# Two stacked graph-attention layers: three more turns by DRAM trips, a round over four graphs, edge counts on ScalarE

## The chip, the cores and the metric

The kernel runs on one core of a Trainium2 chip. The time is the device time of one execution in microseconds (us), the median of three runs. A core has TensorE (PE in the profile, with PEld for its weight loads), VectorE (DVE), ScalarE (ACT), GpSimd (POOL) and SyncE (SP, which here only issues DMAs). Each takes its instructions in program order and waits on semaphores for the others.

## The reference

64 graphs of 256 nodes with 512 features go through two attention layers, each with a layer norm and a ReLU ahead and a residual sum behind. The first layer is itself two attentions: four heads of 256, ELU, then one head of 512. The second has eight heads of 64. All of it is fp32.

```
h = maximum(layernorm(x), 0)
# layer 0: mask = (adj > 0) | eye
xl = h @ W1 ; e = leaky_relu(asrc[i] + adst[j], 0.2) ; attn = softmax over sources of e, masked
z = elu(attn^T @ xl + b1)                      # 4 heads x 256
x = x + (the same with W2, one head of 512, on z) + b2
h = maximum(layernorm(x), 0)
# layer 1: mask = adj > 0, softmax over the second index, 8 heads x 64
x = x + relu(attention(h @ W_proj))
```

## The kernel before

`short_path` does the work; `general_path` is a fallback that runs only if a range test at the end fails, and it does not run here. The graphs are independent. A class `Graph` holds the steps of one graph as methods, and a text named `order` lists the steps of one *round*; every round runs this list, where the number ahead of a step is the offset of the graph it works on ("-1 exp2" in round r is step exp2 of graph r-1). Scheduling is by hand: the list is the program order on every engine. Beside the B + 2 = 66 rounds there are pieces of weight preparation that are dealt out between the steps of rounds 0 and 1.

The steps are these.

- `load`, `stats1`, `norm1`: x and adj come in, VectorE takes mean and variance, GpSimd makes the scale and the offset, ScalarE writes the normed h.
- A left operand of TensorE must be turned (features on partitions). For the first product h goes to DRAM and comes back with its 32-row blocks regrouped (`away1`), then VectorE's 32x32 block transpose finishes the turn (`turn1`, in `back`). For the other two products TensorE itself transposes 128x128 squares through PSUM, and ScalarE moves them to SBUF (`turn2` on z, 16 squares for a graph; `turn3` on the second h, 8 squares).
- Each projection is a Strassen-Winograd product of 2x2 blocks (class `Product`): seven products p1 to p7, with sums of the left blocks by GpSimd (`left`). m1a and m1b are the two halves of h @ W1 (seven products of 4 matmul records each), m2 is z @ W2 (seven of 8), m3 is h @ W_proj (seven of 4). Products p1, p6, p7, p4 accumulate into one PSUM tile `sum`; after p1, p6 and p7 ScalarE copies it out (`kept`), and the next of them can't write before that copy is done. VectorE adds the copies to the other PSUM tiles (`put`, at c22, p2, p3).
- `exp1/2/3` makes the attention factors; they go to DRAM and come back broadcast to all partitions (`spread`). `edges1/2/3` makes one head's weights: ScalarE scales a broadcast row (`wy`), VectorE takes the maximum and the mask (`e`), twice a head.
- `gat1/2/3` multiplies weights and values on TensorE, `out1/2/3` divides by the sum. `out1` also starts the ELU with two ScalarE passes (`ez`: ReLU, Exp), and `elu1` ends it on VectorE.
- `masks` makes the mask of layer 0 and the caps a01 of layer 1 with the count of edges of each row, all on VectorE; `cap3` turns the caps by a DMA transpose.

Of the kernel before, what the change touches and what calls it, by code (L numbers as in the profile page):

```python
# [17 lines left out]
P = 128  # L18
# [19 lines left out]
class Product:  # L38
# [19 lines left out]
    def kept(self, name):  # L58
        s = self.work.tile([P, 268], F32, name=name)
        self.nc.scalar.activation(s[:, :self.n], self.sum[:, :self.n], AF.Copy)  # L60
        return s

    def p1(self):
        self.sum = self.ps_sum.tile([P, 512], F32, name="sum")
        self.product(self.sum, 0, True, False)
        self.s1 = self.kept("s1")
# [10 lines left out]
    def p6(self):  # L77
        self.product(self.sum, 2, False, False)
        self.u2 = self.kept("u2")

    def p7(self):
        self.product(self.sum, 4, False, False)
        self.u3 = self.kept("u3")
# [14 lines left out]
def short_path(ctx, tc, flags, x, adj, w1, att_src1, att_dst1, b1, w2, att_src2, att_dst2, b2, w_proj, w_att,  # L98
# [12 lines left out]
    G = 4  # L111
# [9 lines left out]
    ps_mm = ctx.enter_context(tc.tile_pool(name="ps_mm", bufs=4, space=PSUM))  # L121
    ps_tr = ctx.enter_context(tc.tile_pool(name="ps_tr", bufs=2, space=PSUM))
# [5 lines left out]
    ident = const.tile([P, P], F32, name="ident")  # L128
# [33 lines left out]
    class Norm:  # L162
# [10 lines left out]
        def end(self):  # L173
            ve = small.tile([P, 2, T], F32, name="ve")
            nc.vector.tensor_scalar(ve[:, 0, :], self.mv[:, :, 1], EPS, None, ALU.add)
            nc.vector.tensor_scalar(ve[:, 1, :], self.mv[:, :, 0], -1.0, None, ALU.mult)
            rstd = small.tile([P, T], F32, name="rstd")
            nc.gpsimd.tensor_tensor(rstd, ve[:, 0, :], neg_half, ALU.pow)
            off = small.tile([P, T], F32, name="off")
            nc.gpsimd.tensor_tensor(off, ve[:, 1, :], rstd, ALU.mult)  # L180
            return rstd, off
# [8 lines left out]
    def turn(h, c, pt):  # L190
        for k in range(2):
            for t in range(T):
                nc.tensor.transpose(pt[:, k, t * P:(t + 1) * P], h(t, c + k), ident)  # L193

    def away(h):

        kept = dram.tile([T, 4, P, P], F32, name="kept_h")
        nc.sync.dma_start(kept.rearrange("t a p e -> p t a e"), h.rearrange("p t (a e) -> p t a e", a=4))  # L200
        nc.sync.dma_start(h, kept.rearrange("t a (j q) e -> (a j) t (q e)", q=4))

    def back(h, a):

        for t in range(T):
            nc.vector.transpose(a[:, 4 * t:4 * t + 2].rearrange("p r k (j q) -> p q (r k) j", q=4),  # L206
                                h[:, t].rearrange("p (q c i) -> p q c i", q=4, c=4))
# [9 lines left out]
    def left_of(h, gone):  # L217

        a = work.tile([P, 7, DC // 2, P], F32, name="hs")
        if gone:  # L220
            back(h, a)
        else:
            for r in range(2):
                pt = ps_tr.tile([P, 2, N], F32, name="pt")
                turn(lambda t, c: h[:, t, c * P:(c + 1) * P], 2 * r, pt)
                nc.scalar.activation(a[:, r:r + 5:4], pt.rearrange("p k (t q) -> p t k q", t=T), AF.Copy)
# [3 lines left out]
    def spread(w, heads):  # L230

        kept = dram.tile([heads, P, T], F32, name=f"kept{heads}")
        nc.sync.dma_start(kept.rearrange("h p t -> p h t"), w)
        rows = []
# [41 lines left out]
    class Graph:  # L276


        def __init__(self, b):
            self.b = b  # L280

        def load(self):
            self.xs = io.tile([P, T, D], F32, name="xs")
# [4 lines left out]
        def masks(self):  # L288

            self.mask = work.tile([P, T, N], BF16, name="mask")  # L290
            nc.vector.scalar_tensor_tensor(self.mask, self.ad, 0.0, eye, ALU.is_gt, ALU.max)
            a01 = self.a01 = work.tile([P, T, N], BF16, name="a01", bufs=1)
            nc.vector.tensor_scalar(a01, self.ad, 0.0, None, ALU.is_gt)
            deg = small.tile([P, T], F32, name="deg")
            nc.vector.tensor_reduce(deg, a01, AX.X, ALU.add)
            none = small.tile([P, T], F32, name="none")
            nc.vector.tensor_scalar(none, deg, 0.5, EVEN, ALU.is_lt, ALU.mult)
            for t in range(T):
                nc.vector.tensor_scalar(a01[:, t, :], a01[:, t, :], OPEN, none[:, t:t + 1], ALU.mult, ALU.add)

        def stats1(self):
# [4 lines left out]

            exs = self.exs = small.tile([P, 6 * (H1 + 1 + H3)], F32, name="exs")
            self.ex1 = exs[:, :6 * H1].rearrange("p (i t) -> p i t", t=T)
            self.ex2 = exs[:, 6 * H1:6 * (H1 + 1)].rearrange("p (i t) -> p i t", t=T)
            self.ex3 = exs[:, 6 * (H1 + 1):].rearrange("p (i h t) -> p i h t", i=3, t=T)  # L310
# [7 lines left out]
        def away1(self):  # L318
            away(self.h)

        def turn1(self):
            a = left_of(self.h, True)
# [3 lines left out]
        def cap3(self):  # L326
            self.cap = work.tile([P, T, N], BF16, name="cap")
# [4 lines left out]
        def exp1(self):  # L332
            exps(lambda sl: self.ex1[:, sl].rearrange("p h t -> p t h"), H1, xl1[:, :, 0, :L1], xl1[:, :, 1, :L1])
            self.bc1 = spread(self.ex1[:, 2 * H1:], H1)
            self.zt = [work.tile([P, HF], F32, name=f"z{t}", bufs=1) for t in range(T)]
# [16 lines left out]
        def out1(self, g, t):  # L352
            z = self.zt[t]
            for h, pm in self.pms:
                r = small.tile([P, 1], F32, name="r1")
                nc.vector.reciprocal(r, pm[:, Q:Q + 1])
                sl = slice(h * F1, (h + 1) * F1)
                nc.vector.scalar_tensor_tensor(z[:, sl], pm[:, :Q], r, b1_sb[:, sl], ALU.mult, ALU.add)  # L358

            ez = work.tile([P, 2 * F1], F32, name="ez")  # L360
            nc.scalar.activation(ez, z[:, 2 * g * F1:2 * (g + 1) * F1], AF.Relu, scale=-1.0)  # L361
# [3 lines left out]
        def elu1(self, g, t):  # L365
            z = self.zt[t][:, 2 * g * F1:2 * (g + 1) * F1]
# [3 lines left out]
        def turn2(self, r, k):  # L370
            if r == 0 and k == 0:
                self.a2 = work.tile([P, 7, HC // 2, P], F32, name="h1s", bufs=1)
                self.m2 = Product(nc, ps_sum, ps_mm, work, self.a2, w2_sb, put2)
            pt = ps_tr.tile([P, 2, N], F32, name="pt")
            turn(lambda t, c: self.zt[t][:, c * P:(c + 1) * P], 4 * r + 2 * k, pt)
            nc.scalar.activation(self.a2[:, r:r + 5:4, 2 * k:2 * k + 2], pt.rearrange("p k (t q) -> p t k q", t=T),
                                 AF.Copy)
            if r == 1 and k == 1:
                left(self.a2, HC // 2)

        def exp2(self):
            exps(lambda sl: self.ex2[:, sl].rearrange("p h t -> p t h"), 1, xl2[:, :, 0, :L2], xl2[:, :, 1, :L2])
            self.bc2 = spread(self.ex2[:, 2:3], 1)
# [37 lines left out]

        def turn3(self):
            self.m3 = Product(nc, ps_sum, ps_mm, work, left_of(self.h, False), wp_sb, put3)

        def exp3(self):
# [6 lines left out]
            self.bc3 = spread(self.ex3[:, 2], H3)  # L432
# [15 lines left out]
        def out3(self, a, t):  # L448
# [3 lines left out]
            o = work.tile([P, G, K3], F32, name="o", bufs=4)  # L452
# [18 lines left out]
    def bring(w, src, at, r, by, squares=False):  # L471

        nk, n = w.shape[2], w.shape[3]
        for half in range(2):
            dst = blocks(w)[r][half][:, :, n - Q:]
            cols = src[:, at + half * Q:at + (half + 1) * Q]
            if squares:
                for a in range(4):
                    by[half].dma_start(dst[32 * a:32 * (a + 1)], cols[a * P:(a + 1) * P].rearrange(
                        "(c i) f -> i c f", c=4)[:, r * nk:(r + 1) * nk])  # L480
            else:
                by[half].dma_start(dst, cols.rearrange("(c p) f -> p c f", p=P)[:, r * nk:(r + 1) * nk])
# [385 lines left out]
```

## Time and profile before

| | |
|---|---|
| median of three runs | 3426.02 us (3424.45 to 3426.62) |
| profiled execution: device time | 3423.96 us |
| profiled execution: first to last instruction | 3421.9 us |
| VectorE busy | 2492.3 us, 73% of the span |
| ScalarE busy | 1876.7 us, 55% |
| GpSimd busy | 1231.4 us, 36% |
| DMA, mean share of the 16 engines | 3 tenths, 82 GB/s |

The times come from one profiled execution. "Busy" is the time in which at least one instruction of an engine runs. A group's mean is the length of one instruction; the starts of neighbours lie up to 0.09 us closer than these lengths, because instructions overlap at their ends. "Idle before" says how long the engine stood still ahead of an instruction, and who ended it.

### The profile page before, as it was taken

Reading aid. Unit: us, or ns where it says so; the run is one execution under the profiler, and the core shown is the slowest. Engines: PE = TensorE matmul, PEld = TensorE weight load, DVE = VectorE, ACT = ScalarE, POOL = GpSimd, SP = SyncE. Lnnn points to the kernel's source line nnn. Section 1 sums busy time; section 2 is a strip of 40 time slices with the busy share of each in tenths; the row PEclk is TensorE's granted clock in tenths of the full one; section 3 lists DMA queues with packets and bytes.
Section 4 is the critical chain, followed back from the end, with each engine's and each line's share of the span. In section 5 each row is a group of like instructions: output and inputs, shape, how many; then the busy total and the mean of one; then the engine's idle time right before and its main releaser. Section 6 shows DMA issues by size and latency. Waiting matters only on the chain.

```text
span 3421.9 us, 51905 instructions
## 1 busy us (share of the span) xinstructions
PE 3326.7 (97%) x17668; PEld 2899.3 (85%) x17668; DVE 2492.3 (73%) x6447; ACT 1876.7 (55%) x4481; POOL 1231.4 (36%) x1369
## 2 busy tenths in 40 slices
PE   4899999999999999999999999999999999999997
PEld 3688888888888888888888888888888888888886
DVE  7577777777777777777777777777777777777773
ACT  2355555555555555555565565565565565555553
POOL 1333433333433433433433433433433434334332
PEclk8999999999999999999999999999999999999997
DMA  4223323323223233323323323323223233232331
GB/s 134 58 85 82 82 85 81 83 82 85 83 80 86 81 81 83 85 78 81 90 75 82 92 75 82 90 76 83 86 80 83 81 86 81 80 87 78 84 78 40
DMA packets 354316, 280.87 MB, mean 82 GB/s; under 512 B 159616, under 2 KB 254848, under 8 KB 354048
## 3 DMA queue, kind: packets, MB, share of 16 engines
q1 hardware_dynamic: 352480, 275.40, 29.7%
q8 instruction: 144, 2.36, 0.3%
q10 hardware_dynamic: 1568, 2.10, 0.2%
q14 instruction: 124, 1.02, 0.1%
HBM read 201.07 MB, written 67.96 MB: 79 GB/s over the span
## 4 chain that ended last, share of the span: by engine, by line
PE 88%; ACT 5%; DMA 3%; DVE 2%; issue 1%; POOL 0%; SPq 0%; ACTq 0%; DVEq 0%
PE sum L54 30%; PE pm L54 21%; PE pm L445 13%; PE pm L348 13%; PE pm L399 6%; PE pt L193 5%; ACT wy L273 3%; DMA kept<-exs 1%; DMA bc<-kept 1%; ACT u L60 1%; ACT s L60 0%; DVE wy L492 0%; DMA w1a_sb<-in_L_gnn_W_dram 0%; DVE e L274 0%; POOL o L553 0%
## 5 line engine op out<-in xcount | busy, mean ns | idle before, releaser
L273 ACT ACTIVATE wy<-bc,exs 128x256 f32<-128x256 f32 x1664 | 768.9, 520 | 194.5 <-DMA bc<-kept 79.2
L455 POOL TENSOR_TENSOR x<-x,o 128x256 f32<-128x256 f32 x256 | 197.7, 772 | 1446.0 <-DVE o L453 1446.0
L274 DVE SCALAR_TENSOR_TENSOR e<-wy,exs,cap 128x256 f32<-128x256 f32 x1024 | 486.4, 511 | 141.0 <-ACT wy L273 133.3
L445 PEld LDWEIGHTS pm<-xl,e 128*128 128x128 f32 x4096 | 505.4, 195 | 26.5 <-issue 9.8
L348 PE MATMUL pm<-xl,e 128*128 128x257 f32 x2048 | 496.6, 385 | 9.9 <-DVE e L274 6.5
L445 PE MATMUL pm<-xl,e 128*128 128x65 f32 x4096 | 494.5, 275 | 11.3 <-DVE e L274 11.3
L54 PE MATMUL sum<-w_sb,h1s 128*128 128x257 f32 x2048 | 493.7, 383 | 0.7 <-ACT u L60 0.7
L54 PEld LDWEIGHTS sum<-w_sb,h1s 128*128 128x128 f32 x2048 | 379.9, 190 | 73.6 <-issue 21.8
L246 DVE TENSOR_TENSOR xl<-pm,u 128x256 f32<-128x256 f32 (+2 forms) x512 | 214.8, 419 | 310.0 <-PE pm L54 249.8
L348 PEld LDWEIGHTS pm<-xl,e 128*128 128x128 f32 x2048 | 375.2, 191 | 59.2 <-DVE e L274 8.4
L60 ACT ACTIVATE u<-sum 128x260 f32<-128x260 f32 (+3 forms) x512 | 196.5, 384 | 356.7 <-PE sum L54 350.7
L54 PE MATMUL pm<-w_sb,h1s 128*128 128x257 f32 x1536 | 365.0, 379 | 0.0
L54 PEld LDWEIGHTS pm<-w_sb,h1s 128*128 128x128 f32 x1536 | 290.9, 189 | 43.9
L54 PE MATMUL sum<-w1a_sb,hs 128*128 128x260 f32 x1024 | 274.7, 391 | 36.0 <-DVE hs L206 28.8
L274 DVE SCALAR_TENSOR_TENSOR e<-wy,exs,mask 128x256 f32<-128x256 f32 x640 | 274.7, 476 | 46.9 <-ACT wy L273 46.9
L212 POOL TENSOR_TENSOR hs<-hs 128x256 f32<-128x256 f32 x128 | 93.6, 731 | 543.1 <-DVE hs L206 324.6
L54 PE MATMUL sum<-wp_sb,hs 128*128 128x264 f32 x1024 | 277.3, 393 | 1.2 <-ACT u L60 1.1
L54 PE MATMUL sum<-w1b_sb,hs 128*128 128x256 f32 x1024 | 271.1, 387 | 1.0 <-ACT u L60 1.0
L54 PEld LDWEIGHTS sum<-w1a_sb,hs 128*128 128x128 f32 x1024 | 188.4, 190 | 89.2 <-ACT u L60 32.1
L358 DVE SCALAR_TENSOR_TENSOR z<-pm,r,b_sb 128x256 f32<-128x256 f32 x512 | 247.7, 484 | 18.1
L361 ACT ACTIVATE ez<-z 128x512 f32<-128x512 f32 x256 | 160.4, 627 | 164.9 <-DVE z L358 164.7
L399 PE MATMUL pm<-xl,e 128*128 128x257 f32 (+1 forms) x1024 | 243.8, 381 | 0.8 <-DVE e L274 0.7
(92 smaller groups left out, 5284.7 us busy)
## 6 DMA issues: line engine op xcount, KB each, us to landing
bc<-kept SPq DMA_DIRECT2D x384, 256.0 KB, 3.8
xs<-in_x_dram SPq DMA_DIRECT2D x64, 512.0 KB, 3.9
kept_h<-h SPq DMA_DIRECT2D x64, 512.0 KB, 3.2
h<-kept_h SPq DMA_DIRECT2D x64, 512.0 KB, 3.6
out_dram<-x SPq DMA_DIRECT2D x64, 512.0 KB, 2.8
ad<-in_adj_dram SPq DMA_DIRECT2D x64, 256.0 KB, 4.2
bc<-kept SPq DMA_DIRECT2D x64, 128.0 KB, 4.2
w_sb<-in_L_gnn_W_dram SPq DMA_DIRECT2D x4, 512.0 KB, 9.2
```

The lines of the kernel that those rows point to most:

```text
L54: self.nc.tensor.matmul(to[:, :self.n], self.lhs[:, i, c, :], self.rhs[:, i, c, :], start=(first and c == 0), stop=(last and c == self.nk ...
L60: self.nc.scalar.activation(s[:, :self.n], self.sum[:, :self.n], AF.Copy)
L193: nc.tensor.transpose(pt[:, k, t * P:(t + 1) * P], h(t, c + k), ident)
L246: nc.vector.tensor_tensor(dst, pm, add, ALU.add)
L273: nc.scalar.activation(wy, bc, AF.Copy, scale=yw)
L274: nc.vector.scalar_tensor_tensor(dst, wy.rearrange("p t q -> p (t q)"), xw, mask, ALU.max, op)
L348: nc.tensor.matmul(pm[:, :Q + 1], self.e[1, h][:, s, t * P:(t + 1) * P], xl1[:, s, h, L1:], start=(s == 0), stop=(s == T - 1))
L358: nc.vector.scalar_tensor_tensor(z[:, sl], pm[:, :Q], r, b1_sb[:, sl], ALU.mult, ALU.add)
L361: nc.scalar.activation(ez, z[:, 2 * g * F1:2 * (g + 1) * F1], AF.Relu, scale=-1.0)
L399: nc.tensor.matmul(pm[:, :n], self.e[2][:, s, t * P:(t + 1) * P], xl2[:, s, half, L2:L2 + n], start=(s == 0), stop=(s == T - 1))
L445: nc.tensor.matmul(pv[:, h, :], self.e[3, a * G + h][:, s, t * P:(t + 1) * P], xl3[:, s, a * G + h, :], start=(s == 0), stop=(s == T - 1))
L455: nc.gpsimd.tensor_tensor(to, to, o.rearrange("p h k -> p (h k)"), ALU.add)
```

## The change

The turns of z and of the second h no longer use TensorE. They go the way of the first h: to DRAM (`away2`, `away3`), back (`home2`, `home3`) and through VectorE's block transposes. A trip out is now four DMAs of 32 partitions each, and issuing it and fetching it back are two steps of the list. z is laid out by pairs of heads, so that its two halves travel apart. The broadcast trips are split in the same way: `keep` at the exp step, `spread` at new steps `rows1/2/3`. The round spans four graphs (offsets 1, 0, -1, -2, -3), so there are 67 rounds, and the list is new throughout. The edge counts and the caps move from VectorE to ScalarE, with GpSimd between them; the mask is made from a01 in bf16 and not from the int32 adjacency; the small operations of the norm move from VectorE to GpSimd. PSUM goes from 4 + 2 banks of pm and pt to 5 + 1.

```diff
-    ps_mm = ctx.enter_context(tc.tile_pool(name="ps_mm", bufs=4, space=PSUM))
-    ps_tr = ctx.enter_context(tc.tile_pool(name="ps_tr", bufs=2, space=PSUM))
+    ps_mm = ctx.enter_context(tc.tile_pool(name="ps_mm", bufs=5, space=PSUM))
+    ps_tr = ctx.enter_context(tc.tile_pool(name="ps_tr", bufs=1, space=PSUM))
...
-            nc.vector.tensor_scalar(ve[:, 0, :], self.mv[:, :, 1], EPS, None, ALU.add)
-            nc.vector.tensor_scalar(ve[:, 1, :], self.mv[:, :, 0], -1.0, None, ALU.mult)
             rstd = small.tile([P, T], F32, name="rstd")
-            nc.gpsimd.tensor_tensor(rstd, ve[:, 0, :], neg_half, ALU.pow)
+            nc.gpsimd.tensor_scalar(rstd, self.mv[:, :, 1], EPS, None, ALU.add)
+            nc.gpsimd.tensor_tensor(rstd, rstd, neg_half, ALU.pow)
...
     def away(h):
-        kept = dram.tile([T, 4, P, P], F32, name="kept_h")
-        nc.sync.dma_start(kept.rearrange("t a p e -> p t a e"), h.rearrange("p t (a e) -> p t a e", a=4))
-        nc.sync.dma_start(h, kept.rearrange("t a (j q) e -> (a j) t (q e)", q=4))
+        kept = dram.tile([4, 32, T, 4, P], F32, name="kept_h")
+        for q in range(4):
+            nc.sync.dma_start(kept[:, :, :, q, :].rearrange("a j t e -> j t a e"),
+                              h[32 * q:32 * (q + 1)].rearrange("j t (a e) -> j t a e", a=4))
+        return kept
+
+    def home(h, kept):
+        nc.sync.dma_start(h, kept.rearrange("a j t q e -> (a j) t (q e)"))
...
         def masks(self):
-            self.mask = work.tile([P, T, N], BF16, name="mask")
-            nc.vector.scalar_tensor_tensor(self.mask, self.ad, 0.0, eye, ALU.is_gt, ALU.max)
             a01 = self.a01 = work.tile([P, T, N], BF16, name="a01", bufs=1)
             nc.vector.tensor_scalar(a01, self.ad, 0.0, None, ALU.is_gt)
+            self.mask = work.tile([P, T, N], BF16, name="mask")
+            nc.vector.tensor_tensor(self.mask, a01, eye, ALU.max)
             deg = small.tile([P, T], F32, name="deg")
-            nc.vector.tensor_reduce(deg, a01, AX.X, ALU.add)
+            for t in range(T):
+                same = work.tile([P, N], BF16, name="same", bufs=1)
+                nc.scalar.activation(same, a01[:, t, :], AF.Copy, accum_out=deg[:, t:t + 1])
             none = small.tile([P, T], F32, name="none")
-            nc.vector.tensor_scalar(none, deg, 0.5, EVEN, ALU.is_lt, ALU.mult)
+            nc.gpsimd.tensor_scalar(none, deg, 0.5, EVEN, ALU.is_lt, ALU.mult)
             for t in range(T):
-                nc.vector.tensor_scalar(a01[:, t, :], a01[:, t, :], OPEN, none[:, t:t + 1], ALU.mult, ALU.add)
+                nc.scalar.activation(a01[:, t, :], a01[:, t, :], AF.Identity, bias=none[:, t:t + 1], scale=OPEN)
...
-        def turn2(self, r, k):
...
-            pt = ps_tr.tile([P, 2, N], F32, name="pt")
-            turn(lambda t, c: self.zt[t][:, c * P:(c + 1) * P], 4 * r + 2 * k, pt)
-            nc.scalar.activation(self.a2[:, r:r + 5:4, 2 * k:2 * k + 2], pt.rearrange("p k (t q) -> p t k q", t=T),
-                                 AF.Copy)
...
+        def away2(self, g):
+            self.kept2[g] = away(self.z[:, g])
+
+        def home2(self, g):
+            home(self.z[:, g], self.kept2[g])
+
+        def turn2(self, g):
...
+            for t in range(T):
+                back(self.z[:, g], t, self.a2[:, g + 4 * t])
+            if g == 1:
                 left(self.a2, HC // 2)
...
+        0 m1a p1, -2 stats3 1, -1 elu1 1 1, -1 away2 1, -3 edges3 0, 0 m1a p2, -1 home2 0, 0 m1a p5, -3 edges3 1,
+        0 m1a p6, -2 norm3, 0 m1b p1, -2 away3, -3 edges3 2, 0 m1a p7, 0 m1a c22, -1 home2 1, -3 edges3 3,
+        0 m1b p2, 0 m1a p4, 0 m1a p3, 0 exp1, -1 turn2 0, 0 m1b p6, 0 m1b p5, -2 home3, -3 gat3 0 0, -3 out3 0 0,
+        -3 edges3 4, 0 m1b p7, 0 m1b c22, 0 rows1, 1 load, -1 cap3, -1 turn2 1, -3 gat3 0 1, -3 out3 0 1, -3 edges3 5,
+        -1 m2 p1, 0 m1b p4, 0 m1b p3, -3 edges3 6, -2 turn3, -1 m2 p2, 0 masks, -3 edges3 7, -1 m2 p6, -1 m2 p5,
+        1 stats1, 1 norm1, 1 away1, -3 gat3 1 0, -3 out3 1 0, -1 m2 p7, -1 m2 c22, 1 bias, -3 gat3 1 1, -3 out3 1 1,
+        0 edges1 0, 1 home1, -3 store, -3 range, -1 m2 p4, 0 edges1 1, -1 m2 p3, -1 exp2,
+        -2 m3 p1, 0 edges1 2, -2 m3 p2, -2 m3 p5, 0 edges1 3, -2 m3 p6, 1 turn1, -1 rows2,
+        0 gat1 0 0, 0 out1 0 0, -2 m3 p7, -2 m3 c22, 0 gat1 0 1, 0 out1 0 1, 0 elu1 0 0, -2 m3 p4, -2 m3 p3, -2 exp3,
+        0 gat1 1 0, 0 out1 1 0, 0 elu1 0 1, 0 away2 0, -1 edges2, 0 gat1 1 1, 0 out1 1 1, 0 elu1 1 0, -2 rows3,
+        -1 gat2 0, -1 out2 0, -1 stats3 0, -1 gat2 1, -1 out2 1
...
+    for r in range(B + 3):
```

The old list, which these lines replace, is printed with the kernel above. What is not shown are the loading of the weights in the new block layout, buffer counts (`kept` 4, `xs` 3, `cap` 3, `o` 2), and the flush of the weight pieces at the end of rounds 0 and 1.

## The prediction

> **What bounds the kernel now.** I read the page's busy table first, then its chain of waits, then one steady round by windows, and last the order of time inside that round.
>
> ```profile
> PE 3326.7 (97%) x17668; PEld 2899.3 (85%) x17668; DVE 2492.3 (73%) x6447; ACT 1876.7 (55%) x4481; POOL 1231.4 (36%) x1369
> PE 88%; ACT 5%; DMA 3%; DVE 2%; issue 1%; POOL 0%; SPq 0%; ACTq 0%; DVEq 0%
> PE sum L54 30%; PE pm L54 21%; PE pm L445 13%; PE pm L348 13%; PE pm L399 6%; PE pt L193 5%; ACT wy L273 3%; DMA kept<-exs 1%; DMA bc<-kept 1%; ACT u L60 1%; ACT s L60 0%; DVE wy L492 0%; DMA w1a_sb<-in_L_gnn_W_dram 0%; DVE e L274 0%; POOL o L553 0%
> ```
>
> TensorE carries 88% of the chain, and its transposes (pt L193) are 5% of it: the prize. The chain also shows the round: "PE sum L54 x20" comes back at 152.66 and 204.22, every 51.57 us. The windows of two such rounds (length; busy us of PE, PEld, DVE, ACT, POOL):
>
> ```profile
> 2526.00:2577.57 51.57, 51.48 (x278) 45.02 (x277) 37.94 (x99) 29.21 (x70) 19.07 (x21) 1.00 0.29 83
> 3094.11:3145.69 51.58, 51.48 (x278) 45.02 (x277) 38.31 (x99) 29.27 (x70) 19.06 (x21) 1.00 0.29 82
> ```
>
> So every other engine has slack in total, VectorE least (13 us). What matters is where it falls. The timeline gives the prices of the steps that TensorE waits for:
>
> ```profile
> 2537.22 0.38 ACT L60 ACTIVATE u<-sum 128x260 f32<-128x260 f32 x1
> 2537.65 0.74 PEld L54 LDWEIGHTS sum<-w1a_sb,hs 128*128 128x128 f32 x4 [0.49 <-ACT u L60]
> 2542.64 2.60 ACT L273 ACTIVATE wy<-bc,exs 128x256 f32<-128x256 f32 x6
> 2554.93 0.63 ACT L361 ACTIVATE ez<-z 128x512 f32<-128x512 f32 x1 [1.85 <-DVE z L358]
> 2555.59 0.63 ACT L362 ACTIVATE ez<-ez 128x512 f32<-128x512 f32 x1
> 2557.55 1.52 ACT L186 ACTIVATE h<-x,off,rstd 128x512 f32<-128x512 f32 x2 [1.32 <-POOL off L180]
> 2564.27 1.04 PE L193 MATMUL pt<-ident,z 128*128 128x128 f32 x8
> 2577.39 2.02 DVE L206 STREAM_TRANSPOSE hs<-h 128x512 f32<-128x512 f32 x2 [0.31 <-DMA h<-kept_h]
> ```
>
> The second line is the one to notice: TensorE stood 0.49 us because one ScalarE copy was late, and went on 0.05 us after its end. Before, that costs little since no long ScalarE work is queued ahead of the copies.
>
> **What the Trainium skill says.** "TensorE: Matmul & The Clock Gate", section "Architectural detail: the array is 16× 32×32, not 1× 128×128": ScalarE and VectorE are strict FIFO, and TensorE only pulls weight loads ahead. The trace agrees (the 0.49 us). So a copy queued behind other ScalarE work waits for all of it. "VectorE: DVE Perf Modes", section "The three transpose paths": VectorE's transpose makes 32x32 blocks only, hence the DRAM trip; here two of 128x512 take 2.02 us. "DMA: Bandwidth & Descriptors", section "Anatomy of one DMA": about 2 us of a DMA are fixed; our 512 KB trips land after 3.2 us out and 3.6 back.
>
> **The change, part by part.**
>
> *Removed.* 24 squares a round; a block of eight holds TensorE 0.87 us (2564.27 to the next start, 2565.14), so 2.61 us. The waits for their evictions (hs L226 0.4) and about 0.5 of late copies go too: a floor of 51.57 - 2.61 - 0.9 = 48.1 us. ScalarE loses six evictions (4 x 0.594 + 2 x 0.584 = 3.5 us).
>
> *Added.* VectorE gets six block transposes, 3 x 2.02 = 6.1, and loses the mask on int32 (1.65, back as a bf16 maximum: 0.33 to 0.6, I take 0.4; below by the page's rate for two-input bf16, above by one element a cycle), count 0.69, caps 0.56, norm 0.65, none 0.17: net +2.8, 41 us. ScalarE gets two counts and two caps: "ScalarE: Activation LUTs", section "Step-by-step: what each stage is for", gives 186 + 0.833 N ns, 93 more for a pointer and 93 of overlap: 0.40 each for N = 256, 0.8 + 0.8 = 1.6 us in all. GpSimd's small operations are 0.2 each (off L180, 195 ns), +1.0. DMA: three more trips, 3.1 MB a round beside 4.3 now (280.87 MB / 66): 0.29 goes to about 0.5. SP issues 18 more DMAs of 0.37 to 0.43 us, 7 us on a queue that stands idle most of the round. In total all fits under 48.1 us.
>
> *Moved.* The order of the built kernel decides. I walk from points where TensorE would be on time. Prices: product of m1 or m3 0.87 to 0.89, of m2 1.74, gat step 1.73; PSUM to reader 0.2; copy 0.38; wy 0.44; an e pair 0.9; put 0.4; out1 1.2 (2556.44 to 2557.63); stats of both tiles 1.72; a01 1.46; left of m1/m3 3.3 (L212 to L215: 731 + 889 + 948 + 726 ns).
>
> 1. Start of round. ScalarE has, in order: copy of p6, norm3, copy of m1b p1, wy pair of head 2, copy of m1a p7. From the end of p6: 0.2 + 0.38 + 1.52 + 0.38 + 0.88 + 0.38 = 3.7. TensorE has m1b p1, m1a p7, m1b p2 (2.6) before m1a p4, which accumulates into that PSUM tile. Late 1.1; 1.4 as the copy of p6 is itself behind a fourth wy, whose buffer VectorE frees only after out2, stats3 and elu1.
> 2. Middle. From the end of m1b p3 VectorE has its put, head 6, turn3, m2's p2 put, a01: 0.2 + 0.4 + 0.9 + 2.0 + 0.4 + 1.46 = 5.4. ScalarE counts until 6.2. GpSimd's "none" stands behind left of m3, which began at 3.5: 6.8 + 0.2 = 7.0. Caps 0.85, then the wy pair of head 7, first e at 8.8, second at 9.25. TensorE has m2 p2, p6, p5 and heads 4 to 6 of gat3 1 0: 3 x 1.74 + 1.3 = 6.5, and 0.2 between the halves of head 7. Late 2.6.
> 3. Right after it: stats1 1.72, four GpSimd operations 1.35 (pow is 704 ns), norm1 1.52, then the copy of m2 p7, 0.38: 5.0. TensorE has 0.2 + 1.74 + 1.73. Late 1.3 at m2 p4.
> 4. gat1. turn1 sits ahead of out1, so out1 starts about 0.85 late. From the end of gat1 0 0: 0.2 + 0.85 + 1.2 + ez 1.26 + copy of m3 p7 0.38 = 3.9; TensorE has 0.89 + 1.73. Late 1.3 at m3 p4.
> 5. gat2 needs edges2, and its wy stand behind ez of gat1 1 0: 0.2 + 1.2 + 1.26 + 0.44 + 0.46 = 3.6 from that end, second half 0.45 later; TensorE has 1.73. Late 2.0.
>
> The trips end in time: away2 of the second half is issued by about 5 us of the round, lands at 8, is home at 12; its transposes come at 15. I cost DMA at nothing; with 4 us more it would be late at m2 p2.
>
> The sum: 1.4 + 2.6 + 1.3 + 1.3 + 2.0 = 8.6, so 48.1 + 8.6 = 56.7 us a round, 5.1 over before.
>
> *Ends.* Before: round 2's m1 starts at 154, the 62 rounds from there to the last full one take 62 x 51.57 = 3197, and 70 remain. After: round 0 ends with gat1, which in before ended at 72 (74); round 1 is 64 without m3 (58); round 2 lacks gat3 (46): round 3 starts at 178. Then 61 full rounds. The tail has m2, m3 and gat3 of the last graph one after another, with their trips: before from the end of m2 64; m2 starts about 13 in, takes 19 with what lies between, and m3 has a trip of 8 more: 105. Span 178 + 61 x 56.7 + 105 = 3742; the profiled run took 2 us more than its span and the median 4 more: 3745.
>
> **The rivals.**
>
> *A: the five waits (main case).* Strip the late starts of VectorE and the minima of the five are 1.1 + 2.2 + 1.2 + 0.5 + 1.9 = 6.9: 55.0 a round, 3640. If contention or the doubtful prices add 2 us, 58.7, 3865. Chance 0.68.
>
> *B: half of it.* If TensorE's order lets one wait cover the next (a stall at 2 gives VectorE time that 4 lacks), 52.5: 3486. For it: VectorE's 13 us of slack. Against: 2 and 3 are one chain, not two claims on one gap. Chance 0.12. A tail of this case near 51.5 (the round that breaks even: (3422 - 283) / 61) is no change.
>
> *C: TensorE stays the bound, faster.* One mechanism: the ScalarE work ahead of each copy is ready early, so it has run before TensorE's next product; it decides wherever norm, ez and caps end before the copy's matmul does. Then 48.5 a round: 165 + 61 x 48.5 + 100 = 3224. For it: 97% on TensorE and slack everywhere else. Against: ez follows the gat just ended, and caps follow m2's put, so they cannot be early. Chance 0.15.
>
> *D: trips late.* 3 trips of 6 us on one SP queue that also waits for norms and elu1: 61 a round, 4004. Against: three tenths of DMA busy. Chance 0.05.
>
> That the change doesn't do what it says is out: the built order has no L193 left.
>
> **How the numbers follow.** Likeliest is A: 3745. From 3560 (between A's minimum and B) to 3865. About 0.2% is what a measurement can tell from no change. Faster is C, 0.15; same, 0.03; slower the rest, 0.82.
>
> **What would show it.** Right: a round of 55 to 58 us; PE near 85% busy; TensorE's waits led by "ACT kept" ahead of sum L54 and by "DVE e" ahead of gat2 and gat3; the wy of head 7 right behind the caps; DMA share 0.45 to 0.55. Wrong: PE at 97% still and a round below 50 (C), or VectorE's block transposes waiting for DMA (D). The forecast fails if I mis-ordered a ScalarE queue, or if the counts cost far less.

## The result: 14% slower, 165 us beyond the forecast

| | before | after |
|---|---|---|
| median | 3425.78 us (3424.45 to 3426.62) | 3909.78 us (3905.28 to 3916.73) |
| ratio, with 95% interval | | 1.1415 (1.1395 to 1.1435) |
| profiled execution, first to last instruction | 3421.9 us | 3903.6 us |
| round | 51.57 us | 59.02 us |

The forecast was 3745 us, 3560 to 3865 for the range: the right sign, and too small, with the median 45 us above the range's upper end. After's mean round comes from the timeline: round 4 starts at 256.24 us, the last full one at 3738.38, 59 rounds apart. Round 3 starts at 195.67 (178 was forecast; rounds 1 and 2 start at 79 and 144, for 74 and 132). So of the 162 us by which the span missed its forecast (3903.6 against 3742), 18 lie in the head, some 2 in the tail, and the rest is 61 rounds that are 2.3 us longer than forecast.

The page of after, busy table and two groups (busy us, mean ns of one, idle before and its releaser), and the group of before that answers to the first:

```profile
PE 3336.6 (85%) x16132; PEld 2866.8 (73%) x16132; DVE 2682.4 (69%) x6319; ACT 1766.7 (45%) x4481; POOL 1315.9 (34%) x1689
...
L269 DVE SCALAR_TENSOR_TENSOR e<-wy,exs,cap 128x256 f32<-128x256 f32 x1024 | 697.8, 721 | 270.2 <-ACT wy L268 270.2
...
L466 PE MATMUL pm<-xl,e 128*128 128x65 f32 x4096 | 564.6, 293 | 282.3 <-DVE e L269 282.3
```

```profile
L274 DVE SCALAR_TENSOR_TENSOR e<-wy,exs,cap 128x256 f32<-128x256 f32 x1024 | 486.4, 511 | 141.0 <-ACT wy L273 133.3
```

TensorE went from 97% to 85%, and no other engine took its place: the highest, VectorE, is at 69%. So TensorE waits more; no engine has become full in its place. The e with the cap (L269) is the first surprise: 721 ns on the mean, where before has 511.

The windows of two rounds of after (columns as before: length, busy us of PE, PEld, DVE, ACT, POOL, granted clock, DMA share, GB/s):

```profile
2557.97:2616.13 58.16, 50.85 (x254) 43.85 (x253) 41.51 (x97) 27.41 (x70) 20.43 (x26) 0.97 0.51 128
2854.61:2913.72 59.11, 52.20 (x253) 45.04 (x252) 40.72 (x97) 27.66 (x70) 20.53 (x26) 0.94 0.48 126
```

24 matmul records fewer than the 278 of before should have taken TensorE's busy time from 51.48 to 48.9. It is 51 to 52, because the clock column is no longer 1.00. The rest of the round is waiting. The table of waits (us in total, times, longest):

```profile
PE pm L466 <- DVE e L269: 282.3, 73, 9.2
...
PE sum L54 <- ACT kept L60: 117.4, 110, 4.6
...
DVE a L287 <- DMA cap<-a: 93.7, 59, 3.8
PE pm L411 <- DVE e L269: 92.0, 64, 3.6
```

The first line is head 7 of gat3 1 0, the forecast's middle chain, and it is larger than the other two of TensorE together (4.29 us a round). The third says that VectorE's a01 waited 1.6 us in nearly every round for the caps' DMA transposes, a wait that the forecast did not have. The timeline shows both at their place (start, length, engine and line, operation, in brackets the idle time before it and its releaser):

```profile
2574.63 1.27 POOL L208 TENSOR_TENSOR h1s<-h1s 128x512 f32<-128x512 f32 x1 [1.97 <-DVE r L472]
...
2574.93 2.67 DVE L269 SCALAR_TENSOR_TENSOR e<-wy,exs,cap 128x256 f32<-128x256 f32 x2
...
2575.63 2.79 SPq L325 DMA_TRANSPOSE cap<-a  x2
...
2575.98 1.33 POOL L209 TENSOR_TENSOR h1s<-h1s 128x512 f32<-128x512 f32 x1
...
2577.27 1.45 POOL L210 TENSOR_TENSOR h1s<-h1s 128x512 f32<-128x512 f32 x1
...
2577.85 2.56 DVE L269 SCALAR_TENSOR_TENSOR e<-wy,exs,cap 128x256 f32<-128x256 f32 x2
...
2578.68 1.45 POOL L211 TENSOR_TENSOR h1s<-h1s 128x512 f32<-128x512 f32 x1
...
2582.41 0.43 DVE L287 TENSOR_SCALAR a<-ad 128x512 bf16<-128x512 int32 x1 [0.47 <-DMA cap<-a]
...
2585.20 0.91 ACT L297 ACTIVATE a<-a,none 128x256 bf16<-128x256 bf16 x2 [1.28 <-POOL none L295]
2586.01 0.92 ACT L268 ACTIVATE wy<-bc,exs 128x256 f32<-128x256 f32 x2
2586.55 0.90 DVE L269 SCALAR_TENSOR_TENSOR e<-wy,exs,cap 128x256 f32<-128x256 f32 x2 [2.85 <-ACT wy L268]
...
2587.09 1.12 PE L466 MATMUL pm<-xl,e 128*128 128x65 f32 x4 [3.42 <-DVE e L269]
```

From the bottom up, this is the chain that the forecast named: head 7 waits for its e, e for wy, wy for the caps, the caps for GpSimd's "none". What is new stands above it: two e pairs of 2.67 and 2.56 us, each beside two of GpSimd's sums of m2 (h1s), where a pair without such company takes 0.90 (2586.55). And behind the wait the clock falls:

```profile
2586.00:2587.00 1.00, 0.00 (x0) 0.00 (x0) 0.45 (x2) 1.00 (x4) 0.00 (x0) 1.00 0.00 0
2587.00:2588.00 1.00, 0.91 (x4) 0.91 (x5) 1.00 (x3) 0.20 (x1) 0.00 (x0) 0.54 0.00 0
2588.00:2589.00 1.00, 1.00 (x4) 0.81 (x5) 0.93 (x5) 0.00 (x0) 0.00 (x0) 0.50 0.00 0
2589.00:2590.00 1.00, 1.00 (x4) 0.82 (x3) 0.55 (x3) 0.00 (x0) 0.77 (x2) 0.50 0.00 0
```

The last column but two is the granted clock: half of full. m2 p7, whose eight matmuls begin at 2588.01, took 3.18 us where 1.9 is usual.

### The profile page after: what moved, and what is told of

The parts are those of the page before. It is cut to its first block, busy times and chain, and to the rows that moved or that the text cites. A ratio compares the mean times of both kernels' runs of the same rounds, so it can differ in the third digit from the quotient of the medians.

```text
span 3903.6 us, 50557 instructions
## 1 busy us (share of the span) xinstructions
PE 3336.6 (85%) x16132; PEld 2866.8 (73%) x16132; DVE 2682.4 (69%) x6319; ACT 1766.7 (45%) x4481; POOL 1315.9 (34%) x1689
## 5 line engine op out<-in xcount | busy, mean ns | idle before, releaser
L269 DVE SCALAR_TENSOR_TENSOR e<-wy,exs,cap 128x256 f32<-128x256 f32 x1024 | 697.8, 721 | 270.2 <-ACT wy L268 270.2
L466 PE MATMUL pm<-xl,e 128*128 128x65 f32 x4096 | 564.6, 293 | 282.3 <-DVE e L269 282.3
L466 PEld LDWEIGHTS pm<-xl,e 128*128 128x128 f32 x4096 | 567.5, 212 | 313.5 <-DVE e L269 276.0
L54 PE MATMUL sum<-w_sb,h1s 128*128 128x257 f32 x2048 | 606.4, 447 | 11.5 <-ACT kept L60 9.0
L60 ACT ACTIVATE kept<-sum 128x260 f32<-128x260 f32 (+3 forms) x768 | 289.4, 377 | 499.0 <-PE sum L54 497.5
L54 PEld LDWEIGHTS sum<-w_sb,h1s 128*128 128x128 f32 x2048 | 445.5, 226 | 86.7 <-POOL rstd L175 8.8
L241 DVE TENSOR_TENSOR xl<-pm,kept 128x256 f32<-128x256 f32 (+2 forms) x768 | 318.5, 415 | 229.2 <-ACT kept L60 197.6
L269 DVE SCALAR_TENSOR_TENSOR e<-wy,exs,mask 128x256 f32<-128x256 f32 x640 | 337.8, 565 | 172.2 <-ACT wy L268 171.8
L351 PEld LDWEIGHTS pm<-xl,e 128*128 128x128 f32 x2048 | 389.5, 190 | 77.1 <-DVE e L269 17.0
L476 POOL TENSOR_TENSOR x<-x,o 128x256 f32<-128x256 f32 x256 | 219.7, 858 | 629.0 <-DVE o L474 601.5
L175 POOL TENSOR_SCALAR rstd<-mv 128x2 f32<-128x2 f32 x128 | 50.4, 394 | 1077.0 <-DVE mv L171 838.1
L411 PEld LDWEIGHTS pm<-xl,e 128*128 128x128 f32 x1024 | 189.6, 190 | 141.0 <-issue 115.9
```

Source lines behind the costliest of these rows:

```text
L54: self.nc.tensor.matmul(to[:, :self.n], self.lhs[:, i, c, :], self.rhs[:, i, c, :], start=(first and c == 0), stop=(last and c == self.nk ...
L175: nc.gpsimd.tensor_scalar(rstd, self.mv[:, :, 1], EPS, None, ALU.add)
L241: nc.vector.tensor_tensor(dst, pm, add, ALU.add)
L269: nc.vector.scalar_tensor_tensor(dst, wy.rearrange("p t q -> p (t q)"), xw, mask, ALU.max, op)
L351: nc.tensor.matmul(pm[:, :Q + 1], self.e[1, h][:, s, t * P:(t + 1) * P], xl1[:, s, h, L1:], start=(s == 0), stop=(s == T - 1))
L411: nc.tensor.matmul(pm[:, :n], self.e[2][:, s, t * P:(t + 1) * P], xl2[:, s, half, L2:L2 + n], start=(s == 0), stop=(s == T - 1))
```

## The experiments

Seventeen kernels ran. Where no interval is given, a kernel ran once, beside 3426 or 3432 us for the kernel before. "Round" is worked out as above, from the same two points of each trace.

### Which part of the change costs what

Three kernels undo the change part by part. In the first, only the turns of z and of the second h go back to TensorE:

```diff
-            for t in range(T):
-                back(self.z[:, g], t, self.a2[:, g + 4 * t])
+            for k in range(2):
+                pt = ps_tr.tile([P, 2, N], F32, name="pt")
+                for c in range(2):
+                    for t in range(T):
+                        nc.tensor.transpose(pt[:, c, t * P:(t + 1) * P], self.z[:, g, t, ...], ident)
+                nc.scalar.activation(self.a2[:, g:g + 5:4, 2 * k:2 * k + 2], pt..., AF.Copy)
```

> One part undone: the turns of z and of the second h are again TensorE transposes with ScalarE evictions at the places of turn2 and turn3 in the new list (PSUM 4 + 2 banks again); the four-graph list, counts, caps and mask stay as changed. TensorE gets 2.6 us a round more, VectorE loses 4.1, SP 15 DMAs. If TensorE's time adds to the waits, 3904 + 61 x 2.6 = 4060. If TensorE's new work fits into its waits because another engine's cycle sets the round, 3780 to 3900. If the trips themselves are what the change pays for, 3600 or less.

3786.47 us (3785.80 to 3789.88), ratio 1.1053 (1.1036 to 1.1070). TensorE has 2.6 us a round more to do, and the kernel is 123 us *faster* than after: the wait at head 7 is gone (20 us in the whole run):

```profile
L478 PE MATMUL pm<-xl,e 128*128 128x65 f32 x4096 | 523.8, 278 | 19.8 <-DVE e L277 19.8
```

So TensorE did have room for its own transposes, in its waits.

The second also takes mask, counts, caps and the norm's small operations back to VectorE, so that of the change the list is left, with what goes with it (broadcasts and the first h's trip split in two steps, more buffers, the new layout of the block transposes):

> Only the four-graph list is left of the change: the turns of z and of the second h on TensorE, mask, counts and caps and the small norm operations on VectorE as before; the broadcast fetches stay steps of their own. Turns on TensorE alone gave 3786. If the counts and caps on ScalarE and GpSimd are what lengthens that kernel's rounds (its waits for ScalarE's copies are 3.2 us a round), 3600 or less. If the list itself costs them, because the copies stand behind norm1, norm3 and ez wherever the counts are, 3700 to 3800.

3707.74 us (3706.99 to 3710.38), ratio 1.0806 (1.0790 to 1.0823), round 55.88. Its waits:

```profile
PE sum L54 <- ACT kept L60: 147.3, 190, 5.0
PE pm L422 <- DVE e L278: 91.2, 64, 2.8
```

These are the copies late behind norm3, norm1 and ez, and gat2 late behind the wy of edges2: chains 1, 3, 4 and 5 of the forecast, here 0.72, 0.55, 0.97 and 1.39 us a round. They belong to the list and come without any of the new trips. So of the 14.2% loss, taken apart in this order, the list makes 8.1, the mask, counts, caps and norm 2.5, and the trips, with all that they save TensorE and with the PSUM banks, 3.6.

The third undoes only the counts and caps, with trips and list as changed:

```diff
-                nc.scalar.activation(same, a01[:, t, :], AF.Copy, accum_out=deg[:, t:t + 1])
+            nc.vector.tensor_reduce(deg, a01, AX.X, ALU.add)
...
-            nc.gpsimd.tensor_scalar(none, deg, 0.5, EVEN, ALU.is_lt, ALU.mult)
+            nc.vector.tensor_scalar(none, deg, 0.5, EVEN, ALU.is_lt, ALU.mult)
...
-                nc.scalar.activation(a01[:, t, :], a01[:, t, :], AF.Identity, bias=none[:, t:t + 1], scale=OPEN)
+                nc.vector.tensor_scalar(a01[:, t, :], a01[:, t, :], OPEN, none[:, t:t + 1], ALU.mult, ALU.add)
```

> Only counts, none and caps go back to VectorE, with all else as changed. Theory 1: from the end of a01 to head 7's first e it is 2.7 us in place of 4.2, so the wait shrinks to about 2.8 and most of the half clock goes: 55.5 us a round, 3690 in all (3650 to 3800[...]). Theory 2: 3900 or more, VectorE has more work.

3851.4 us, round 58.03; the wait at head 7 went from 4.29 to 3.33. So going over three engines with the counts cost about 1 us a round; most of the wait is not theirs. The kernel that makes no new trips (it leaves out the trips of z and of the second h, and the block transposes turn what is there, so the output differs) says how little of it is transfer time:

> Left out: the trips of z and of the second h through DRAM (15 of the 18 added DMAs and the two homes of z and the one of h); the block transposes work on rows that are not regrouped, so the left sides are other numbers. Theory 1 (trips are covered): only the wait of a01 for the cap DMA, up to 1.5 us a round, can shorten: 3800 to 3904. Theory 2 (trips are what makes TensorE late): 3500 or less.

3846.75 us, round 58.11, head 7 still 3.37, with a DMA share of 0.30. The transfers are worth 1 us a round; VectorE's block transposes remain, and so does the wait.

### The wait at head 7

Order alone first. With `0 masks` behind `-3 edges3 7`:

> The step masks is moved one place back in the list, behind edges3 7, so that head 7's wy pair no longer stands behind the counts and caps on ScalarE. Theory 1 (the wait of TensorE for head 7, 4.3 us a round, is made by counts and caps, and the clock that is halved after it costs some 3 us more): the wait for head 7 falls under 0.5 us and the clock stays whole; about 2.5 us come back at m2 p7, since the copy of m2 p6 is now behind the caps. A round of 54.2 us, 3610 in all. Theory 2 (the new DRAM trips make TensorE late): nothing moves but the place of the wait, 3850 to 3904.

3878.97 us, round 58.47. The wait at head 7 fell to 0.31, and 3.31 us came up at m2 p7, which waits for the copy of m2 p6 behind counts and caps on ScalarE: the same chain, met one product later. With counts and caps as a step of their own behind `0 out1 1 1`:

> The counts, none and caps become a step of their own near the end of the round, behind out1 of the last gat1 step, where ScalarE has no copy due; a01 and the mask stay where they are. Theory 1 (the five chains of the forecast): head 7's wait falls from 4.3 to about 0.4, no half clock, and nothing lands on the copy of m2 p6; chain 3 (norm1 ahead of the copy of m2 p7) comes out with up to 1.3 and the gat1 copy with 1.0. A round of 53.5 us, about 3570. Theory 2 (the round is set by VectorE and GpSimd colliding, 41 us of VectorE that can't be packed tighter): over 56 us a round, 3720 or more.

3801.86 us, round 57.25, head 7 still 2.42. That is the best of the changes by order, and a third of what I expected of it. Two others are the caps' transposes at the head of the round,

> Only the step cap3 moves: to the head of the round, ahead of away2, and so off SP's place behind rows1 and load. If the surplus of the wait for head 7 over the forecast (4.3 against 2.6) comes from a01 waiting for the caps' DMA behind rows1 on SP (1.5 us a round), that wait falls to 2.8, with less of the half clock: a round of 57 us or less, 3780. If it comes from the e pairs that take 2.6 us beside GpSimd's sums for m2, the wait falls by less than 0.5, since a01 is then late by itself: 3870 to 3904.

and GpSimd's four sums of m2 left out, the products reading raw blocks:

> Left out: the four GpSimd sums of m2's left blocks (5.3 us a round); the products take raw blocks in their place, so the output is another one. If e pairs of 2.6 us beside these sums make head 7 late: e with caps goes from 721 to about 530 ns, the wait for head 7 from 4.3 to under 2.5, 3750 or less. If a01 is held by the caps' DMA: e gets as fast, but a01 then waits longer for the DMA, head 7's wait stays above 3.5, 3850 to 3904.

3885.59 and 3898.25 us: next to nothing, both. The groups of VectorE tell why. The early caps:

```profile
L269 DVE SCALAR_TENSOR_TENSOR e<-wy,exs,cap 128x256 f32<-128x256 f32 x1024 | 698.0, 721 | 305.6 <-ACT wy L268 305.6
...
L287 DVE TENSOR_SCALAR a<-ad 128x512 bf16<-128x512 int32 x64 | 57.6, 899 | 0.0
```

And the kernel without the sums:

```profile
L271 DVE SCALAR_TENSOR_TENSOR e<-wy,exs,cap 128x256 f32<-128x256 f32 x1024 | 510.7, 539 | 273.5 <-ACT wy L270 273.5
...
L289 DVE TENSOR_SCALAR a<-ad 128x512 bf16<-128x512 int32 x64 | 28.2, 441 | 241.7 <-DMA cap<-a 241.7
```

With the caps early, a01 waits for no DMA, but e is as slow as ever, and a01, which now falls beside GpSimd's sums of m3, takes 899 ns where after has 624. Without the sums e is at 539 ns, but VectorE now stands at a01 for the caps' DMA, 241.7 us in all instead of 93.7. Two delays side by side: whichever goes, the other is reached. So both at once:

> The caps' DMA transposes at the head of the round, and GpSimd's four sums of m2 left out (the products take raw blocks in their place, so the output differs). Each alone gave 6 to 18 us. If the two causes stand side by side and each hides the other, the wait at head 7 falls from 4.3 us to below 2.5 and the time to 3790 or less; if the head 7 wait comes from the counts and caps chain itself, 3860 to 3885.

3726.95 us (3722.46 to 3732.62), ratio 1.0880 (1.0864 to 1.0897): 183 us less than after, where the two alone gave 24 and 12. The wait at head 7 is 1.52 us a round, the round 56.12:

```profile
L467 PE MATMUL pm<-xl,e 128*128 128x65 f32 x4096 | 534.7, 281 | 113.5 <-DVE e L271 113.5
```

The chain can be measured in two pieces, as means over 59 or 60 rounds of the timeline, in us: from the start of m2 p2 on TensorE (the point where the forecast's walk begins) to the start of a01, and from there to the start of head 7's first e.

| | to a01 | from a01 to e | wait at head 7 |
|---|---|---|---|
| forecast | 3.9 | 4.4 | 2.6 |
| after | 6.8 | 3.7 | 4.3 |
| caps early | 5.5 | 4.6 | 3.8 |
| without m2's sums | 6.9 | 3.2 | 4.1 |
| both | 3.0 | 4.7 | 1.5 |

To see whether the sums have to be left out for it, they were put on VectorE (the caps early too):

```diff
-    def left(a, nk):
+    def left(a, nk, by=nc.gpsimd):
...
-                left(self.a2, HC // 2)
+                left(self.a2, HC // 2, nc.vector)
```

> The changed kernel with the caps' DMA transposes at the head of the round and m2's four sums on VectorE instead of GpSimd; nothing is left out. If what cost the time was that VectorE's e and GpSimd's sums take turns, e with the cap falls from 720 ns to about 540, VectorE pays some 4 x 0.6 = 2.4 us a round for the sums itself, in front of m2 where they are on the path: 3727 + 61 x 0.6 to 61 x 2.4, 3760 to 3870, below the 3886 of the early caps alone. If the sums cost VectorE as much as they held it up, 3886 or more.

3866.62 us (3865.36 to 3872.09), ratio 1.1265 (1.1248 to 1.1283). e fell to 539 ns as expected: 16 in a round save 16 x 0.18 = 2.9 us. The sums take VectorE 4 x 0.69 = 2.8, and the wait at head 7 is back at 3.65 us. So GpSimd's sums take from VectorE about what they would cost on it; by these runs the time is only to be had if neither stands ahead of head 7.

The Trainium skill agrees on the e: "SBUF — State Buffer", section "Who interferes with whom", says that a VectorE instruction with two SBUF inputs contends with a GpSimd instruction that reads SBUF, and calls the ports that they share an exclusive lock. Here e has wy and cap as inputs, and pairs took 2.67 and 2.56 us beside sums of 1.27 to 1.45 us, 0.90 without.

All moved by order, with counts and caps apart, the caps early and a01 behind edges3 7:

> The changed kernel with the middle chain taken apart by order alone, no instruction removed: counts and caps as a step of their own behind out1 1 1, a01 and mask behind edges3 7, the caps' DMA transposes at the head of the round. If the forecast only mis-sized the middle chain (4.3 us instead of 2.6, made longer by the a01 that waits for the caps' DMA), taking it away alone gives what caps apart gave and the 2.4 us that were left at head 7 there: 57.25 - 2.4 = 54.9 us a round, 3660 (3620 to 3720). If the round is set by a cycle through VectorE, ScalarE and the DMA queue, so that a wait taken away comes back elsewhere, 3760 or more.

3812.07 us (3801.85 to 3819.16), ratio 1.1119 (1.1100 to 1.1138), round 57.64: the rival's 3760 or more, and not the 3660. Head 7 is down to 0.41, and m2's copies are late by 2.74 in its place. And with all five chains worked on at once, in a list of my own:

> Caps apart as before, and the list taken through the five chains: norm3 behind the copy of m1a p7, norm1 behind the copy of m2 p7, gat3 1 0 behind m2 p7, out1 behind c22 of m3, edges2 ahead of out1 of the third gat1 step, turn1 into the end of the round, cap3 ahead of rows1. No instruction is taken away. Theory 1: all five waits go but for some tenths; 50 us a round, 3340 (3290 to 3400), which beats the kernel before. Theory 2: still over 55 us a round, 3650 or more, whatever the order.

3869.95 us (3859.98 to 3881.75), ratio 1.1282 (1.1252 to 1.1311), where the first theory had 3340: the largest miss. The five chains as I had named them were gone; new ones stood there. Three lines of its table of waits:

```profile
ACT wy L268 <- DMA bc<-kept: 239.6, 116, 7.4
...
DVE h1s L203 <- DMA z<-kept_h: 107.8, 59, 4.2
...
PE sum L54 <- POOL h1s L209: 36.2, 29, 1.7
```

The broadcasts and the trips of z came late on SP, and copies stood behind the wy that waited for them. I did not find a list in which all of this fits, which is no proof that there is none.

### TensorE's clock behind a wait

Eight idle matmuls ahead of head 7, into a PSUM tile that nothing reads, keep TensorE busy in its longest wait:

> Eight idle matmuls of 128x256 (two passes of 0.216 us each, 3.5 us) on weights that are there anyway are put ahead of head 7 of the second gat3 step, into a PSUM tile that nobody reads; they fill the wait and compute nothing. Theory 1 (after 3.4 to 5.5 us without work TensorE runs at half clock for a while, some 3 us a round): m2 p7 goes from about 3 us back to 1.8, the mean clock from 0.94 to above 0.98, about 3720 in all, though TensorE has more to do. Rival (m2 p7 is slow because of its own operands): 3904, or up to 200 more.

3906.82 us, where about 3720 was expected: the mean clock is 0.979 instead of 0.938, and the time lies within the scatter of after's runs. Other waits came up: m2 p4 for its copy 1.09 us a round (none in after), m3 p4 0.91 (0.55), and 0.8 was left at head 7. So in this kernel the slow running mostly fills time in which TensorE would stand at the next chains.

### One trip in the old list

If it is the list that costs, a single trip in the kernel before should pay. Four kernels send the second h through DRAM and leave z on TensorE (all four also make the mask from a01, the second too, whose expectation says otherwise; only the first has the four-part trips and the new layout of the block transposes). In the first, the fetch of the next graph's h was put behind exp3:

> The kernel before with its own list of three graphs, but the turn of the second h goes through DRAM: stats3 and norm3 moved ahead of edges1 3, the fetch and the block transposes where VectorE has room, turn2 of the first half moved ahead of m3. Eight TensorE squares a round fewer; VectorE gets two block transposes (in the faster layout, for the first h too) and the mask from a01. If a trip that is issued early costs nothing and it is the new list that costs, 8 x 0.109 x 63 = 55 us less: 3370 (3350 to 3400). If a trip costs VectorE or latency wherever it stands, 3430 or more.

4628.88 us (4625.42 to 4636.98), ratio 1.3511 (1.3492 to 1.3529), 70.9 us a round from store to store. The queue of SP shows my slip:

```profile
2643.18 2.57 SPq L201 DMA_DIRECT2D kept_h<-h  x4
2649.10 0.38 SPq L238 DMA_DIRECT2D kept<-exs  x1
2653.34 1.76 SPq L243 DMA_DIRECT2D bc<-kept  x4
2655.27 0.32 SPq L206 DMA_DIRECT2D h<-kept_h  x1
```

The first line sends h away, the last fetches it. Between them SP waits for exp3's factors and then until they have landed, 12 us after h went out. m1a p1 waited 9.4 us for that fetch in the same round: one DMA in the wrong place of a queue. With out and fetch together, and more of TensorE's work ahead of m3:

> The kernel before with one trip, in another order than the one-trip run: out and fetch issued together, ahead of the caps' transposes, so that no broadcast stands between them on SP; stats3 and norm3 behind edges1 3; gat3 1 1 behind gat1 1 1 and all of turn2 ahead of m3, so that TensorE has work for the trip's 7 us; mask and transposes as before. If a trip with its latency covered costs nothing: 62 x 0.87 = 54 us less, 3372 (3355 to 3400). If norm3 ahead of ez or the block transposes on VectorE put a new wait into gat1 or m3, 3426 or more.

3922.74 us (3920.69 to 3925.80), ratio 1.1432 (1.1416 to 1.1447). The trip was in time, but the next graph's norm stood behind m2's sums on GpSimd, and copies behind that norm. With the statistics ahead of those sums:

> The kernel before with one trip (second h), its statistics of the next graph now ahead of m2's sums on GpSimd, norm1 and its trip ahead of m3, norm3 behind the first ez. If nothing is late any more: 54 us less than before, 3372; if turn2 still waits about 1 us a round for ez and its evictions, 3372 + 62 = 3434; if the trip takes another wait with it, 3500 or more.

3814.14 us (3812.89 to 3830.12), ratio 1.1116 (1.1101 to 1.1132). TensorE's waits were down to 3.9 us a round, yet rounds took 57.9 us (from store to store, over 58 rounds). Its windows:

```profile
2634.00:2636.00 2.00, 0.64 (x6) 0.40 (x4) 1.90 (x7) 1.97 (x4) 0.36 (x1) 1.00 0.54 32
2636.00:2638.00 2.00, 1.42 (x7) 1.26 (x8) 1.53 (x5) 0.23 (x2) 1.52 (x3) 0.69 0.91 296
2638.00:2640.00 2.00, 1.67 (x5) 1.06 (x5) 1.83 (x2) 1.10 (x3) 0.21 (x2) 0.50 0.45 170
2640.00:2642.00 2.00, 2.00 (x6) 1.58 (x5) 0.00 (x0) 1.71 (x3) 1.92 (x3) 0.50 0.25 92
```

The longest wait of this round is 1.73 us, for elu1, and behind it the clock is at half for about 6 us. With gat3 1 1 and m2 p1 moved into the gaps:

> The kernel before with one trip, and the two gaps of the run with norm1 first filled by order alone: gat3 1 1 and m2 p1 between the halves of turn2 and m3, no product of m3 right behind the copy it waits for. That run's recorded waits were some 2.7 us a round, yet its round was 57.4 us: behind the 1.7 us wait TensorE ran at 0.55 to 0.6 of its clock for about 8 us. If that slow running hangs on the wait, both go together: 3380 to 3430. If the slow running comes from elsewhere (more DMA, more VectorE work), the round stays above 55 us: 3650 or more.

3632.70 us (3626.79 to 3639.36), ratio 1.0582 (1.0568 to 1.0596), 54.9 us a round. Of the 3.1 us a round that it won over the run ahead of it, 0.9 are waits of TensorE (3.0 us a round for 3.9, over the same 58 rounds) and 2.2 are TensorE's busy time (51.7 for 53.9), the slow running: the mean clock of these rounds is 1.00 for 0.94. So the slow running went with the long wait, though the order around it changed too. It still loses to the kernel before, mostly by the waits that are left. No version here beats that kernel.

## Why the forecast was right in sign and short in size

The forecast's own sum for a round, set beside what the trace of after has, in us:

| step of the forecast | forecast | measured |
|---|---|---|
| floor: TensorE without its 24 squares | 48.1 | 48.9 |
| 1. start of round, m1a p4 | 1.4 | 1.18 |
| 2. middle, head 7 | 2.6 | 4.29 |
| 3. m2 p4 | 1.3 | 0 |
| 4. m3 p4 | 1.3 | 0.55 |
| 5. gat2 | 2.0 | 1.39 |
| TensorE below full clock | not in the sum | 2.7 |
| round | 56.7 | 59.0 |

The floor's 48.9 is worked out, 51.48 of before less 2.61 for the squares. The last term is TensorE's busy time in the window of the 59 rounds, 3043.4 / 59 = 51.6, less that floor. Of the 2.3 us that the round is too long, step 2 makes 1.7, the floor 0.8, the clock with steps 3 and 4 together 0.65, and steps 1 and 5 give back 0.8.

*The step that failed is 2, the middle*, in its first half: "head 6, turn3, m2's p2 put, a01" at prices from rows of before. It took "an e pair 0.9", the price of a pair with no GpSimd sum beside it; the last pair ahead of a01, head 6's, took 2.56 us on the mean in after, and the put ahead of that pair starts 0.7 us late, behind head 5's pair, which is as slow. And it let a01 start as soon as VectorE was free, where a01 waited 1.45 us (mean of the full rounds) for the caps' DMA, which stands on SP behind the broadcasts and the loads. These three are 3.8 us; turn3 at 1.3 for 2.0 and shorter steps give some back, and a01 starts 2.9 us later than forecast. Behind it the chain is shorter, 3.7 for 4.4, since a01 took 0.62 us and not 1.46. Shown: with both delays away a01 starts at 3.0 and the round is 56.1 us. That the time is then 3727, so near the forecast's 3745, has some luck in it, since other terms differ too.

*Steps 3 and 4* were right as chains and did not show as waits in full, since TensorE came to them slowly. The idle matmuls brought them out, 1.09 and 0.91 for 1.3 and 1.3, and with the turns on TensorE, at a mean clock of 0.98, they were 1.15 and 0.76. The forecast had no term for the clock at all; in this kernel that term and those two steps largely stand in each other's place (2.7 for 2.6, less the 0.55 that is left at m3 p4).

*Steps 1 and 5* held in kind, at 1.18 for 1.4 and 1.39 for 2.0, and they are there with the list alone (0.72 and 1.39).

*The floor* was 0.8 too low. "The waits for their evictions (0.4) and about 0.5 of late copies go too" cannot be: the windows that the forecast quotes have TensorE busy for 51.48 of 51.57 us, so only 0.09 were there to go. *VectorE's total* came as forecast, 41.2 us a round for 41, but with luck in it: its eight block transposes took 5.2 us a round, where the forecast's price makes 8.1, and its e took 4.3 more than in before.

*The trips* "at nothing" held to 1 us a round for the transfers (the run without them), but their block transposes sit on VectorE ahead of head 7: without the transfers that wait is still 3.37, with TensorE doing the turns it is gone (there TensorE also comes to head 7 later, by its squares). And a trip out holds SP, ahead of the caps' DMA, for 2.6 us, 0.62 for each of its four DMAs, where the forecast took 0.37 to 0.43. *ScalarE's prices* held: the Trainium skill, "ScalarE: Activation LUTs", section "What ACT_TABLE_LOAD costs", gives 186 + 0.833 N ns and 93 more for a pointer, an estimate of 0.40 and 0.49 us for N = 256; a count took 0.42, with 0.19 more for reading the accumulator, which the forecast lacked, and a cap 0.50. *The head* was 18 us longer than forecast, 5 to 6 in each of rounds 0 to 2; the cause stays open.

Of the rivals, C (TensorE stays the bound, faster) is refuted by 85% on TensorE, B by a round of 59 where it needed 52.5, and D, late trips, by the run without the new ones. D's sign did show, though small: VectorE's block transposes waited for DMA for 72 us in the whole run, 12 in before. The DMA share, 0.48 to 0.52, and TensorE's 85% came as forecast.

## What to carry to other kernels

A saving on the bound engine is only worth what the new order leaves of it: price the list by itself first, by walking each strict queue from the points where the bound engine would be on time. When work moves beside other work, a duration from the old trace no longer holds: here e and a01 took two to three and a half times as long next to GpSimd's sums. And where a wait stays after one cause is gone, try the two likeliest causes together before dropping either.

## What the hardware showed that I had not expected

- The clock. The Trainium skill, "TensorE: Matmul & The Clock Gate", section "HAM oscillation — how this bites in real kernels", states that idle gaps above some 3.4 us bring TensorE to half clock. The wait of 3.42 us in after agrees (0.50 to 0.54 behind it). But half clock also followed a wait of 1.73 us behind eight transposes, while 1.72 us behind m2 p1 in the last run left the clock at 1.00. What makes the difference was not tried.
- VectorE's block transpose of 128x512 took 1088 ns on the mean in before, where it writes every fourth element of a row, and 686 in after, where 32 elements of a block lie side by side. Among the kernels with one trip, which share before's list in the main, the one with the new layout has 688 and the next two, with the old one, 1090 and 1084.
- a01 (128x512, int32 to bf16) took 417 ns in the second kernel with one trip, where nothing of GpSimd ran beside it, 624 in after, partly beside m3's sums, and 1455 in before, beside m2's. So the forecast's 1.46 for it already held company.
- A count on ScalarE is two instructions: 0.42 us and a read of the accumulator of 0.19.
